# Two-layer graph attention and mixture-of-experts kernel: dense expert products summed from PSUM, nine result buffers, and another order of turns and results at the end

## The chip, the cores and the metric

The kernel runs on one core of a Trainium2 chip. The metric is device time in microseconds (us), the median over several executions. The engines are TensorE (PE, matrix products; PEld is its weight load), VectorE (DVE), ScalarE (ACT), GpSimd (POOL) and SyncE (SP). Each runs its own instructions in order and waits on semaphores for the others. SP issues the plain transfers, POOL the indirect ones (rows chosen by an index).

## What is computed

The input is 64 batches of 256 rows of 256 numbers in float32. Two layers follow each other, each an attention over a fixed graph of 256 nodes and then a feed-forward part:

```python
x = x + elu(attention_4_heads(layernorm(x), adj))     # layer 0
x = x + layernorm(x) @ weight.T + bias
x = x + relu(attention_1_head(layernorm(x), adj))     # layer 1
t = layernorm(x)                                      # tokens, 16384 rows
probs = softmax(t @ router_w.T)                       # 8 experts
rw, re = top_k(probs, 2); rw = rw / rw.sum()
out = t
for e in range(8):
    h = gelu(t @ w1[e] + b1[e])
    out = out + combine[:, e] * (h @ w2[e] + b2[e])   # combine: rw at re, else 0
return x + out
```

## The kernel before

**Batches.** Each batch passes through the attention and feed-forward parts in SBUF (`batch_layers`). At its end it has the normalized rows `xng`, and `base`, the sum of x and the normalized rows, to which the two chosen experts' outputs are still to be added.

**Routed batches.** For 62 of the 64 batches `base` is written to the output in DRAM (L585). The rows are sorted by expert: after a chunk of batches `route` sends every row, with its index and weights, by an indirect DMA to a region of its expert in the DRAM scratch `xs` (L877). Rows are then taken from there in pairs of blocks, 256 rows of one expert each: 131 pairs in all. `expert_pair` loads a pair's rows `xr` (L726) and their indices and weights `xt` (L737), and the expert's first weight matrix `we` (L752); DVE turns the rows blockwise into `sT` (L116, `turned`); `hidden` makes `hT` = gelu of the first product (PE L783, ACT L789); `result` makes the second product `py` in a PSUM bank (L798) and DVE adds the bias into a buffer `y` (L804); ACT scales it by each row's weight (L776). `scatter` adds the two halves of `y` to the output's rows by two indirect DMAs with addition on POOL's queue (L815). Each of them waits for the two of the pair before (`before = added[-2:] + based`), since two pairs can hold the same row. A buffer `y` is free when its scatter has landed.

**Dense batches.** The last two batches (62 and 63) aren't sorted. All 8 experts are computed on all of their rows (`dense_expert`, 16 in all): `hidden`, `result` into a buffer `y`, and then two DVE operations which multiply `y` by the rows' weight for this expert and add it to `base` in SBUF (L843). After the last expert `base` is written out (L850); for batch 63 that write waits for all scatter-adds, as filling rows of incomplete pairs point at its rows.

**Order.** The order of all instructions is written out by hand. Work is cut into pieces by generators: each `yield r` ends a piece and gives the rank r of the next one. The program goes in steps; in each step every active job gives one piece, in order of rank (a negative rank asks for another piece in the same step). Every third step begins a batch; in the steps between, pairs (two for each batch while batches still begin, `more`; three afterwards) and dense experts (two each third step) begin. One scatter is placed per step, at rank 97. A pair begun in step a loads in step a, loads `we` in a+1 (rank 90), is turned in a+2 (rank 95), goes through `hidden` in a+4 (rank 30), through `result` in a+5 (rank 80), and is scaled in a+6. So the turns of one group of pairs fall in the same step as the results of the group before.

**Buffers.** `WBUFS, XBUFS, YBUFS` are the counts of buffers for `we`, `xr` and `y`. `me` (the masked scores of layer 1, written by ACT at L432, read by DVE at L443) has the work pool's 2, `lg` (router scores of a chunk, L603) has 10, `xt` 12, and `w` (the rows' weights) 8.

Of the kernel before, what the change touches and what calls it, by code (L numbers as in the profile page):

```python
# [9 lines left out]
F32 = mybir.dt.float32  # L10
I32 = mybir.dt.int32
AF = mybir.ActivationFunctionType
ALU = mybir.AluOpType
AX = mybir.AxisListType

P = 128
# [11 lines left out]
def kernel(  # L28
# [17 lines left out]
    nc = tc.nc  # L46
    B, N, D = x.shape
    E = router.shape[0]
# [3 lines left out]
    NT = N // P  # L52
# [16 lines left out]
    ROW = D + 4  # L69
# [4 lines left out]
    work = ctx.enter_context(tc.tile_pool(name="work", bufs=2))  # L74
    small = ctx.enter_context(tc.tile_pool(name="small", bufs=4))
    keep = ctx.enter_context(tc.tile_pool(name="keep", bufs=1))
# [170 lines left out]


    C_B1, WROW = KT * D, KT * D + 64
    WBUFS, XBUFS, YBUFS = 7, 5, 7  # L250
    wpack = tc.dram_tile([E, P, WROW], F32, name="wpack")
    w2s = const.tile([P, E, KT * D], F32, tag="w2s", name="w2s")
    b2s = const.tile([P, E, D], F32, tag="b2s", name="b2s")
# [158 lines left out]
    def projected1(xT, rstd, b):  # L412

        q = q1s[b % 2]
        pqs = []
        for t in range(NT):
            pq = bank("pq", [D + 3])
            for k in range(KT):
                nc.tensor.matmul(  # L419
                    pq, xT[:, k, t * P : (t + 1) * P], wx1[:, k, :],  # L420
                    start=(k == 0), stop=(k == KT - 1),
                )
            pqs.append(pq)
        ex = small.tile([P, NT, 3], F32, tag="ex1", name="ex1")
        for t, pq in enumerate(pqs):
            nc.scalar.activation(ex[:, t, :], pq[:, D:], AF.Exp, scale=rstd[:, t : t + 1])
            nc.scalar.activation(
                q[:, t, :D], pq[:, :D], AF.Copy, scale=rstd[:, t : t + 1]
            )
        me = work.tile([P, NT, N], F32, tag="me", name="me")  # L430
        for j in range(NT):
            nc.scalar.activation(me[:, j, :], masks[1][:, j, :], AF.Copy, scale=ex[:, j, 0:1])  # L432
        return q, ex, me
# [276 lines left out]
    def expert_pair(j, n, ids, ef, regs, needs):  # L710

        i = j % GROUP
        upto = min(j + GROUP, n)
        if i == 0:
            _, regs["e"] = nc.values_load_multi_w_load_instructions(
                ids[0:1, 0, j:upto], engines=[mybir.EngineType.SP], min_val=0, max_val=E - 1,
                skip_runtime_bounds_check_because=WHY,
            )
            _, regs["t"] = nc.values_load_multi_w_load_instructions(
                ids[0:1, 1, j:upto], engines=[mybir.EngineType.SP], min_val=0, max_val=E * CAP,  # L720
                skip_runtime_bounds_check_because=WHY,
            )
        e_sp, t_sp = regs["e"][i], regs["t"][i]
        xr = io.tile([P, PAIR // S, KT * S], F32, tag="xr", name="xr", bufs=XBUFS)
        loads = [
            nc.sync.dma_start(  # L726
                out=xr[g * S : (g + 1) * S],
                in_=xs_d.rearrange("(t c q) f -> t q c f", c=PAIR // S, q=S)[
                    bass.ds(t_sp, 1), :, :, g * KT * S : (g + 1) * KT * S
                ].rearrange("t q c f -> (t q) c f"),  # L730
            )
            for g in range(P // S)
        ]

        xt = small.tile([P, 2, ROW - D], F32, tag="xt", name="xt", bufs=12)
        loads.append(
            nc.sync.dma_start(  # L737
                out=xt,
                in_=xs_d.rearrange("(t k p) c -> t p k c", p=P, k=2)[
                    bass.ds(t_sp, 1), :, :, D:  # L740
                ].rearrange("t p k c -> (t p) k c"),
            )
        )
        for load in loads:
            tc.add_to_no_dep_group("rows", load.ins)
            for name in needs:
                tc.add_manual_dep(
                    load.ins, name, AFTER, reason="any sent row may lie in the pair"
                )
        yield 90  # L750
        we = io.tile([P, WROW], F32, tag="we", name="we", bufs=WBUFS)
        nc.sync.dma_start(  # L752
            out=we, in_=wpack[bass.ds(e_sp, 1), :, :].rearrange("e p c -> (e p) c")
        )
        yield 95
        xT = turned(work.tile([P, KT, PAIR], F32, tag="sT", name="sT", bufs=3), xr)
        w = small.tile([P, 2], F32, tag="w", name="w", bufs=8)
        yield 30
        yield 30
        hT = hidden(xT, we)  # L760
        yield -65
        nc.vector.scalar_tensor_tensor(
            w[:, :, None], xt[:, :, 1:2], ef[:, j : j + 1], xt[:, :, 2:3],
            op0=ALU.is_equal, op1=ALU.mult,
        )
        nc.vector.tensor_tensor(w[:, :, None], w[:, :, None], xt[:, :, 3:4], ALU.add)
        yield 80
        if i == 0:
            _, regs["x"] = nc.values_load_multi_w_load_instructions(
                ids[0:1, 0, j:upto], engines=[mybir.EngineType.PE, mybir.EngineType.DVE],  # L770
                min_val=0, max_val=E - 1, skip_runtime_bounds_check_because=WHY,
            )
        y = result(hT, bass.ds(regs["x"][i], 1))
        yield 2
        for t in range(2):
            nc.scalar.activation(y[:, t, :], y[:, t, :], AF.Copy, scale=w[:, t : t + 1])  # L776
        scatters.append((y, xt))
# [13 lines left out]
            )  # L791
        return hT

    def result(hT, e):
        py = bank("py", [2, D])
        for t in range(2):
            for f in range(KT):
                nc.tensor.matmul(  # L798
                    py[:, t, :], hT[:, f, t * P : (t + 1) * P],
                    w2s[:, e, f * D : (f + 1) * D].rearrange("p e c -> p (e c)"),  # L800
                    start=(f == 0), stop=(f == KT - 1),
                )
        y = io.tile([P, 2, D], F32, tag="y", name="y", bufs=YBUFS)
        nc.vector.tensor_add(y, py, b2s[:, e, :].to_broadcast([P, 2, D]))  # L804
        return y
# [25 lines left out]
    def dense_expert(b, e):  # L831

        own = dense_batch[b]
        yield 90
        we = io.tile([P, WROW], F32, tag="we", name="we", bufs=WBUFS)
        nc.sync.dma_start(out=we, in_=wpack[e])
        yield 40
        yield 30
        hT = hidden(own["xT"], we)
        yield 80  # L840
        y = result(hT, slice(e, e + 1))
        for t in range(NT):
            nc.vector.scalar_tensor_tensor(  # L843
                own["base"][:, t, :], y[:, t, :], own["w"][:, t, e : e + 1],
                own["base"][:, t, :], op0=ALU.mult, op1=ALU.add,
            )
        if e == E - 1:
            while b == B - 1 and (scatters or len(added) < 2 * PAIRS):
                yield 99
            d = nc.sync.dma_start(  # L850
                out=out_rows[b * N : (b + 1) * N, :].rearrange("(t p) d -> p t d", p=P),
                in_=own["base"],
            )
            before = added[-2:] + based if b == B - 1 else []
            tc.declare_no_dep(
                d.ins, query=SYNC, group="out", keep=before,
                reason="no row is added to here, or every add is in their chain",
            )
            for ins in before:
                tc.add_manual_dep(d.ins, ins.name, AFTER, reason="filling rows were added here")  # L860
            tc.add_to_no_dep_group("out", d.ins)
            nc.sync.nop()
# [153 lines left out]
    def jobs():  # L1016
        b = done = taken = 0
        for c, nb in enumerate(CHUNKS + (1,) * DENSE):
            nt = nb * NT
            lg = keep.tile([P, nt, E], F32, tag="lg", name=f"lg_{c}", bufs=10)  # L1020
            xng = []
            row0 = b * N
            done += nt
            n = max(done - (E - 1) - taken, 0) if b < ROUTED else 0
            taken += n
            for i in range(nb):
                def job(b=b, c=c, i=i, nb=nb, nt=nt, n=n, lg=lg, xng=xng, row0=row0):
                    yield from batch_layers(b, i * NT, xng, lg)
                    if i == nb - 1:
                        if b >= ROUTED:  # L1030
                            yield 65
                            yield from route_dense(b, lg)
                        else:
                            yield from route(c, row0, nt, n, b == ROUTED - 1, xng, lg)
                yield job()
                b += 1

    batches = jobs()
    step, more, credit = 2, True, 0.0
# [74 lines left out]
```

## Time and profile before

| | us |
|---|---|
| median of 3 runs | 1666.84 |
| lowest and highest | 1666.26, 1670.07 |
| the profiled execution | 1670.08 |
| its span, first to last instruction | 1668.3 |

| engine | busy us | share of the span |
|---|---|---|
| PE | 1495.5 | 90% |
| PEld | 1311.2 | 79% |
| DVE | 1317.4 | 79% |
| POOL | 889.4 | 53% |
| ACT | 833.2 | 50% |

The transfers move 209.74 MB in 365285 packets, of which 264376 are under 512 bytes. The largest groups of transfers are the pairs' rows (524 of 64 KB), the experts' weights (147 of 288 KB), the scatter-adds (262) and the sends (248).

In lines in order of time the first number is the start in us from the start of the span, the second the duration; in brackets stands how long the engine was idle before, and what released it. Releasers are inferred from semaphore events: for a wait on several semaphores the last one is named, and it need not be the one that mattered. L12 is line 12 of the kernel. In a list of waits the numbers are the sum in us, the number of waits and the longest one.

### The profile page before, as it was taken

The numbers are of one execution on the slowest core, as the hardware profiler recorded it, in microseconds if no ns is written. First come the engines' busy times: TensorE is split into PE (matmuls) and PEld (weight loads), VectorE is DVE, ScalarE is ACT, GpSimd is POOL, SyncE is SP. The second block draws the span as 40 slices with busy tenths as digits, with TensorE's granted clock in tenths as the row PEclk, the third lists the DMA queues.
The fourth block names the chain that finished last, engine by engine and source line by source line (L and its number), as shares of the span: only waits on it lengthen the run. The fifth ranks groups of instructions, "written<-read, shape, count | busy, mean of one in ns | idle before, by whom it ended". The sixth has DMA issues, their size and how long they took to land.

```text
span 1668.3 us, 30242 instructions
## 1 busy us (share of the span) xinstructions
PE 1495.5 (90%) x8474; PEld 1311.2 (79%) x8474; DVE 1317.4 (79%) x4478; ACT 833.2 (50%) x1832; POOL 889.4 (53%) x853
## 2 busy tenths in 40 slices
PE   5898888899999999999999999999989987678782
PEld 4777777688888888888888888888878876567671
DVE  6888989999898988898989898998889876423330
ACT  0243444455656666666666665655555565323221
POOL 0121433545757575757575757574764666444344
PEclk8999999999999999999999999999999998879986
DMA  3812223255757575756575766665564676866753
GB/s 107 231 41 58 61 70 94 74 142 114 167 118 163 118 159 129 140 132 146 133 149 134 145 133 146 137 140 121 123 142 99 115 156 141 200 135 112 155 107 44
DMA packets 365285, 209.74 MB, mean 126 GB/s; under 512 B 264376, under 2 KB 335040, under 8 KB 365120
## 3 DMA queue, kind: packets, MB, share of 16 engines
q1 hardware_dynamic: 314496, 139.43, 34.0%
q0 software_dynamic: 49632, 67.39, 22.5%
q8 instruction: 70, 1.15, 0.3%
q10 hardware_dynamic: 992, 0.99, 0.2%
q14 instruction: 95, 0.78, 0.2%
HBM read 118.55 MB, written 89.15 MB: 124 GB/s over the span
## 4 chain that ended last, share of the span: by engine, by line
PE 55%; DVE 26%; DMA 6%; issue 5%; POOL 4%; ACT 2%; SPq 1%; DVEq 0%; POOLq 0%; ACTq 0%
PE ph L783 14%; PE pv L475 12%; PE py L798 9%; PE pq L384 5%; PE pq L419 4%; DVE z L461 4%; PE pf L529 4%; DVE stats L353 4%; DMA out_dram<-y,xt 3%; PE pt L368 3%; POOL out_dram L815 2%; DVE mv L354 2%; PE pl L599 2%; PE pd L454 1%; DVE x L535 1%
## 5 line engine op out<-in xcount | busy, mean ns | idle before, releaser
L815 POOL DMA_INDIRECT out_dram<-y,xt x262 | 416.7, 1591 | 255.4 <-DMA out_dram<-y,xt 73.0
L475 PE MATMUL pv<-q,z 128*128 128x65 f32 (+1 forms) x2560 | 369.8, 299 | 6.7 <-DVE z L461 5.3
L475 PEld LDWEIGHTS pv<-q,z 128*128 128x128 f32 x2560 | 331.9, 194 | 19.5 <-DVE z L461 5.8
L783 PE MATMUL ph<-sT,we 128*128 128x256 f32 x1048 | 259.1, 405 | 56.2 <-DVE sT L116 47.1
L361 POOL TENSOR_SCALAR rstd<-mv 128x4 f32<-128x4 f32 (+1 forms) x132 | 69.7, 528 | 436.1 <-DVE mv L354 352.9
L877 POOL DMA_INDIRECT xs<-xng,pos x248 | 251.1, 1012 | 69.2 <-issue 66.9
L783 PEld LDWEIGHTS ph<-sT,we 128*128 128x128 f32 x1048 | 209.8, 205 | 90.9 <-DVE sT L116 50.6
L798 PE MATMUL py<-w2s,hT 128*128 (+1 forms) x1176 | 263.9, 379 | 1.4 <-DVE z L461 0.7
L798 PEld LDWEIGHTS py<-w2s,hT 128*128 128x128 f32 x1176 | 219.7, 190 | 29.7 <-DVE z L461 1.0
L374 ACT COPY xT<-pt 128x512 f32<-128x512 f32 x192 | 113.3, 590 | 222.4 <-PE pt L368 184.7
L804 DVE TENSOR_TENSOR y<-py,b2s 128x512 f32<-128x512 f32 x147 | 97.5, 688 | 158.9 <-PE py L798 88.7
L789 ACT ACTIVATE hT<-ph,we 128x256 f32<-128x256 f32 x294 | 122.8, 471 | 183.3 <-PE ph L783 80.9
L461 DVE SCALAR_TENSOR_TENSOR z<-pd,q,mask 128x256 f32<-128x256 f32 x512 | 211.1, 473 | 0.3 <-PE pd L454 0.2
L362 POOL TENSOR_TENSOR rstd<-rstd,mhalf 128x4 f32<-128x4 f32 (+1 forms) x132 | 162.6, 1232 | 11.0
L776 ACT ACTIVATE y<-y,w 128x256 f32<-128x256 f32 x262 | 113.1, 501 | 104.4 <-DVE y L804 96.3
L353 DVE BATCH_NORM_STATS2 stats<-x 128x6 f32<-128x256 f32 x384 | 156.3, 407 | 2.2
L384 PE MATMUL pq<-wx,xT 128*128 128x268 f32 x512 | 137.9, 415 | 8.6 <-DVE wt L257 4.2
L419 PE MATMUL pq<-wx,xT 128*128 128x259 f32 x512 | 129.1, 394 | 15.5 <-ACT xT L374 11.2
L529 PE MATMUL pf<-wfT,xT 128*128 128x256 f32 x512 | 125.0, 388 | 0.0
L419 PEld LDWEIGHTS pq<-wx,xT 128*128 128x128 f32 x512 | 91.9, 189 | 41.9 <-ACT xT L374 22.4
L384 PEld LDWEIGHTS pq<-wx,xT 128*128 128x128 f32 x512 | 100.9, 202 | 30.1 <-issue 6.9
L551 ACT ACTIVATE rel<-pv,rinv 128x256 f32<-128x256 f32 x128 | 54.0, 474 | 108.2 <-DVE rinv L482 95.8
(151 smaller groups left out, 2233.8 us busy)
## 6 DMA issues: line engine op xcount, KB each, us to landing
we<-wpack SPq DMA_DIRECT2D x147, 288.0 KB
xr<-xs SPq DMA_DIRECT2D x524, 64.0 KB
xblk<-in_x_dram SPq DMA_DIRECT2D x256, 64.0 KB
xin<-in_x_dram SPq DMA_DIRECT2D x64, 256.0 KB
out_dram<-base SPq DMA_DIRECT2D x64, 256.0 KB
out_dram<-y,xt POOLq DMA_INDIRECT x262
xs<-xng,pos POOLq DMA_INDIRECT x248
xs<-fill SPq DMA_DIRECT2D x9, 260.0 KB
```

The source lines that it names most:

```text
L353: nc.vector.bn_stats(stats[:, t, :], src[:, t, :])
L362: nc.gpsimd.tensor_tensor(rstd[:, :n], rstd[:, :n], mhalf[:, :n], ALU.pow)
L384: nc.tensor.matmul(pq.rearrange("p h c -> p (h c)"), xT[:, k, t * P : (t + 1) * P], wx[:, k, :], start=(k == 0), stop=(k == KT - 1),)
L419: nc.tensor.matmul(pq, xT[:, k, t * P : (t + 1) * P], wx1[:, k, :], start=(k == 0), stop=(k == KT - 1),)
L461: nc.vector.scalar_tensor_tensor(z[:, j, :], pd[:, i, :], q[:, j, h, d + 2 : d + 3], mask[:, j, :], op0=ALU.max, op1=ALU.mult,)
L475: nc.tensor.matmul(pv[:, h, :], z[:, j, t * P : (t + 1) * P], q[:, j, h, : d + 1], start=(j == 0), stop=(j == NT - 1),)
L529: nc.tensor.matmul(pf[:, t, :], xT[:, k, t * P : (t + 1) * P], wfT[:, k, :], start=(k == 0), stop=(k == KT - 1),)
L783: nc.tensor.matmul(ph[:, f, :], we[:, k * D + f * P : k * D + (f + 1) * P], xT[:, k, :], start=(k == 0), stop=(k == KT - 1),)
L789: nc.scalar.activation(hT[:, f, :], ph[:, f, :], AF.Gelu, bias=we[:, C_B1 + f : C_B1 + f + 1])
L798: nc.tensor.matmul(py[:, t, :], hT[:, f, t * P : (t + 1) * P], w2s[:, e, f * D : (f + 1) * D].rearrange("p e c -> p (e c)"), start=(f == 0 ...
L815: d = nc.gpsimd.indirect_dma_start(out=out_rows, out_offset=bass.IndirectOffsetOnAxis(ap=xt[:, t, 0:1].bitcast(I32), axis=0), in_=y[:, t, ...
L877: d = nc.gpsimd.indirect_dma_start(out=xs_d[: E * CAP * PAIR, :], out_offset=bass.IndirectOffsetOnAxis(ap=at, axis=0), in_=xe, in_offset=None,
```

## The change

- `dense_expert` takes the second product straight from PSUM: in place of one add of the bias into `y` and two weighted sums from `y`, there are four weighted sums, two from the PSUM bank and two from the bias rows. No dense expert takes a buffer `y`. The matrix products are split off from `result` into `product`.
- `YBUFS` goes from 7 to 9.
- The turn of a pair has rank 75 in place of 95 once no batch is left to begin, so it comes ahead of the results (rank 80) of the same step.
- The write of a dense batch's `base` comes one step later, at rank 99.
- `me` has 1 buffer in place of 2, `lg` 7 in place of 10, `xt` 14 in place of 12, `w` 12 in place of 8.

```diff
-    WBUFS, XBUFS, YBUFS = 7, 5, 7
+    WBUFS, XBUFS, YBUFS = 7, 5, 9
...
-        me = work.tile([P, NT, N], F32, tag="me", name="me")
+        me = work.tile([P, NT, N], F32, tag="me", name="me", bufs=1)
...
-        xt = small.tile([P, 2, ROW - D], F32, tag="xt", name="xt", bufs=12)
+        xt = small.tile([P, 2, ROW - D], F32, tag="xt", name="xt", bufs=14)
...
-        yield 95
+
+        yield 95 if more else 75
         xT = turned(work.tile([P, KT, PAIR], F32, tag="sT", name="sT", bufs=3), xr)
-        w = small.tile([P, 2], F32, tag="w", name="w", bufs=8)
+        w = small.tile([P, 2], F32, tag="w", name="w", bufs=12)
...
-    def result(hT, e):
+    def product(hT, e):
         py = bank("py", [2, D])
...
+        return py
+
+    def result(hT, e):
+        py = product(hT, e)
         y = io.tile([P, 2, D], F32, tag="y", name="y", bufs=YBUFS)
         nc.vector.tensor_add(y, py, b2s[:, e, :].to_broadcast([P, 2, D]))
         return y
...
-        y = result(hT, slice(e, e + 1))
-        for t in range(NT):
-            nc.vector.scalar_tensor_tensor(
-                own["base"][:, t, :], y[:, t, :], own["w"][:, t, e : e + 1],
-                own["base"][:, t, :], op0=ALU.mult, op1=ALU.add,
-            )
+        py = product(hT, slice(e, e + 1))
+        for t in range(NT):
+            for add in (py[:, t, :], b2s[:, e, :]):
+                nc.vector.scalar_tensor_tensor(
+                    own["base"][:, t, :], add, own["w"][:, t, e : e + 1],
+                    own["base"][:, t, :], op0=ALU.mult, op1=ALU.add,
+                )
         if e == E - 1:
+            yield 99
             while b == B - 1 and (scatters or len(added) < 2 * PAIRS):
                 yield 99
...
-            lg = keep.tile([P, nt, E], F32, tag="lg", name=f"lg_{c}", bufs=10)
+            lg = keep.tile([P, nt, E], F32, tag="lg", name=f"lg_{c}", bufs=7)
```

## The prediction

> **What bounds the kernel now.** I read the table of windows first, for where the engines stop being full; then POOL and DVE in order of time over the last 260 us; then the waits and the DMA queues of that stretch.
>
> ```profile
> 800.00:1000.00 200.00, 197.85 (x1180) 177.09 (x1179) 180.07 (x594) 124.39 (x270) 127.00 (x120) 1.00 0.63 136
> ...
> 1450.00:1500.00 50.00, 31.10 (x122) 25.93 (x121) 13.60 (x33) 9.94 (x24) 21.65 (x14) 0.80 0.67 127
> ```
>
> The columns after the length are busy us of PE, weight load, DVE, ACT and POOL, then clock, DMA share and GB/s. Until about 1330 us TensorE is full (99% here). The tail is another regime: PE is busy 31 of 50 us, DVE 14, and nothing looks full. What does bound it is in POOL's order of time:
>
> ```profile
> 1494.28 1.54 POOL L815 DMA_INDIRECT out_dram<-y,xt  x1 [3.48 <-DMA xr<-xs]
> 1496.13 1.54 POOL L815 DMA_INDIRECT out_dram<-y,xt  x1 [0.31 <-issue]
> 1502.73 1.54 POOL L815 DMA_INDIRECT out_dram<-y,xt  x1 [5.06 <-ACT hT L789]
> ...
> 1625.64 1.54 POOL L815 DMA_INDIRECT out_dram<-y,xt  x1 [3.15 <-DMA out_dram<-y,xt]
> 1627.48 1.54 POOL L815 DMA_INDIRECT out_dram<-y,xt  x1 [0.30 <-issue]
> 1632.08 1.54 POOL L815 DMA_INDIRECT out_dram<-y,xt  x1 [3.05 <-ACT hT L789]
> ...
> 1658.29 1.54 POOL L815 DMA_INDIRECT out_dram<-y,xt  x1 [2.99 <-DMA out_dram<-y,xt]
> ```
>
> Two of these lines are one pair's scatter-add. The code makes each wait for both of the pair before it (L811 to L825: `before = added[-2:]`), so pairs form a chain. Uncontended a link takes 1632.08 - 1625.64 = 6.44 us (1.54 + 0.30 + 1.54 issued, 3.05 to land); beside loads it takes up to 8.45 (1494.28 to 1502.73) or 9.61. Is the chain ever short of data? DVE's order tells:
>
> ```profile
> 1614.28 0.69 DVE L804 TENSOR_TENSOR y<-py,b2s 128x512 f32<-128x512 f32 x1 [11.58 <-PE py L798]
> ...
> 1632.43 0.69 DVE L804 TENSOR_TENSOR y<-py,b2s 128x512 f32<-128x512 f32 x1 [6.81 <-PE py L798]
> 1634.21 0.69 DVE L804 TENSOR_TENSOR y<-py,b2s 128x512 f32<-128x512 f32 x1 [1.09 <-PE py L798]
> 1635.94 0.69 DVE L804 TENSOR_TENSOR y<-py,b2s 128x512 f32<-128x512 f32 x1 [1.03 <-PE py L798]
> ```
>
> The last of 131 pairs is summed at 1635.94 and scattered at 1658.29. Counting both lists back from the end, every pair is ready long before its turn: the least lead from 1440 on is 11.4 us (summed 1614.28, scattered 1625.64; about 1.6 of it go to ACT's scaling). So the chain of adds is the bound from 1405 us on, and DVE and PE wait for it, not it for them:
>
> ```profile
> DVE y L804 <- DMA out_dram<-y,xt: 28.1, 8, 6.2
> ...
> PE ph L783 <- DVE sT L116: 37.2, 7, 9.8
> ```
>
> (waits of 1436 to 1606 us). Those 28.1 us are DVE waiting for a y buffer that a scatter still holds; the turns stand behind it and PE behind the turns. That the releaser column names ACT or a load in POOL's lines is only which event came last by inference.
>
> **What the Trainium skill says.** "DMA: Bandwidth & Descriptors", Issuing engines are not separate DMA queues: transfers of SP and POOL run on the same 16 engines and interleave. The trace agrees: links beside loads are longer. The same page, Rules for kernel authors: an accumulating DMA reads its destination and writes it later, so the next one on the same bytes must wait for its semaphore; the chain must stay, and the diff leaves it. "Perfetto Trace Analysis", Optimization Strategy: the same gap repeating can mean too few buffers; the 28.1 us agree, though here the engine with the gap isn't the one that binds.
>
> **The change part by part.** The chain's sum first. From 1436.73 to 1606.09 there are 23 links in 169.4 us. Links with no load in them take 6.36 to 6.61, mostly 6.45; 23 x 6.45 = 148.4, so loads cost 21.0 us there. The SP queue moved this meanwhile:
>
> ```profile
> q1 hardware_dynamic: 37149, 16.96, 42.0%
> ```
>
> so 21.0/16.96 = 1.24 us per MB, and link by link the excess follows the megabytes (none: 6.45; 0.76 MB: 7.18; 1.72 MB: 8.45; 1.88 MB: 9.61). After 1606 eight links take 52.2 us, then 10.0 us to the end of the span (issue, landing, the last base write). Before 1436 POOL alternates sends (4 x 1.3 us), rstd and scatters in one order that the diff doesn't touch.
>
> (1) *Dense products summed from PSUM.* 16 dense experts lose an add of 0.69 us each (-11.0) and gain two scalar-tensor-tensor of 0.48 (L843; L461 with a PSUM operand takes 0.473) each: 32 x 0.48 = +15.4. DVE gains 4.4 us of work in 170 us where it is 55 busy; PE's bank is held 1.9 rather than 0.7 us, out of 8 banks, with no waiter behind it for most of a round. On the path: 0. If this cover were gone, 4.4.
>
> (2) *Nine y buffers, none for dense.* Of seven, two were taken by dense experts in every round of 3 pairs and 2 experts. Now a sum waits only for the scatter nine pairs earlier: the 28.1 us go. In the whole time before 1400 the same wait is 4.5 us in 6 pieces, DVE being 90% and PE 99% busy; between 0 and -4.5, I take -2.
>
> (3) *Turns at rank 75 instead of 95 once all batches have begun* (the last block turn is at 1293.26). DVE's order in a round becomes 3 turns, 3 pair sums, 2 dense sums; PE then finds sT ready when its products end. Its bubbles before ph (37.2 us) go; a round needs 5.45 + 3.62 + 8.80 = 17.9 us of PE instead of the 21 to 23 us it takes. The last sum would come up to 35 us earlier than 1636. What is late next is the chain, already late: value 0. Between 1310 and 1405 the turns come 1.9 us earlier per round (three sums of 0.6); PE waited 1.67 and 5.79 us there, but POOL's fixed order of sends and scatters ends last: 0, at best -2.
> New wait: if a turn waits for its xr load, three pair sums and two dense ones queue behind it. Loads are issued 10 us or more before their turns (1490.43 for the turn of 1512.03), and the third xr load of a round is released by the first turn of the round before, a whole round ahead. Cost 0 while the 11.4 us lead covers it.
>
> (4) *`yield 99` before the base write of batch 62.* SP stood 14.8 us at L850 for the last dense sum, with two we loads, three pairs' xr and xt, and three we loads behind it. These go out earlier: 0 for the chain. For batch 63 the write still follows the last scatter.
>
> (5) *me with one buffer, lg with 7, xt 14, w 12.* ACT's next me waits for DVE's z of the batch before; over all 64 batches it starts at least 12.1 us after that z began: 0, and each us beyond would cost up to 62 us in all. lg is written and read on DVE alone, 7 chunks apart: 0. The longer xt and w rings remove waits of 0.4 us: 0.
>
> So the only way for (2) to (4) to reach the end is contention. All loads still run; they are squeezed into fewer us. If the price is per MB, as the links show, the 21 us stay, earlier. Bounds: a saturating price could save a third to all of it (-7 to -21); a queue that is never empty could cost half more (+10). I take 0.
> Sum against the profiled execution: 1670.08 - 2 = 1668; this one is 3.2 us above the median of the runs, so on the median 1666.84 - 2 = 1665.
>
> **Rivals.**
> *A, contention saturates:* 2.21 MB in one link (1421.19 to 1429.50) cost only 8.31 us, 1.86 over 6.45, 0.84 us per MB. If all 17 MB ran so, 21.0 becomes 14.3; -7, with (2) at its best -4.5: about 1655. For: those were large packets. Against: 9.61 us for 1.88 MB.
> *B, slower, turns that wait for loads hold the sums up:* place: DVE before three sums of each round in the tail. Per round 5 x 288 KB + 3 x 260 KB = 2.2 MB; the stretch 1436 to 1606 moved 0.1 MB per us, so at that rate a round is 22 us. With sums bound to the next round's loads and loads to the freed buffers, a round could become 24.5 us; 8 rounds x (24.5 - 21.5) = 24, less the 10 us of lead: +14, 1681. It decides from about 22.8 us per round. Against: DMA was at a share of 0.70, the loads waited for buffers, not the buffers for loads.
> *C, the rounds don't quicken* because loads bind them: the chain is fed all the same; no change, 1667.
>
> **How the numbers follow.** No change that shows (the forecast and C): 0.50, own range 1662 to 1671. A: 0.36, from 1645 to 1661. B: 0.14, from 1672 up. About 0.3% (5 us) is what a measurement of this kernel can tell from no change. Predicted 1665; the range goes down to 1650 (the inner part of A) and up to 1671, leaving out some 8% below and 12% above.
>
> **What would show it.** Right: 36 pairs of scatters still follow each other at a mean of about 7.1 us from 1405 on; PE's wait for sT gone; the last pair sum 20 us or more before 1636 while the last scatter stays near 1658; loads ended by about 1580; no wait of ACT before me. Wrong: a mean link under 6.9 (A), DVE waiting at L116 for xr and pairs ready less than 3 us before their scatter (B), or time won before 1330 us, where I see none but the 4.5 us.

## The result, and the profile after

| | before | changed |
|---|---|---|
| median, us | 1666.32 (10 runs) | 1669.78 (10 runs) |
| the profiled execution, us | 1670.08 | 1669.61 |
| its span, us | 1668.3 | 1667.8 |

The ratio is 1.0028, with a 95% interval of 1.0015 to 1.0041 (the quotient of the two medians is 1.0021); a second measurement on another chip (e15) gave 1.0028 again (1.0015 to 1.0041, 1673.59 against 1668.76 us). The change costs about 4 us: little, but clear of the noise. The two profiled spans don't show it, since the first profile of the kernel before is the slowest of these ten runs; a second one (experiment e8) has a span of 1661.7 us. Both run the same chain of adds at the end, and the first is 6 us late when it gets there.

So from here the stretch before the 94th pair's scatter, which varies from execution to execution, is kept apart from the chain that follows it. A *link* is the time from the first scatter of a pair to the first of the next. All 131 pairs were numbered in POOL's order of time.

| profile | 94th scatter at | 94th to last | 98th to last | excess per MB, 98th to last |
|---|---|---|---|---|
| before | 1386.2 | 272.1 | 237.1 | 1.16 |
| before, second profile (e8) | 1380.4 | 271.5 | 236.6 | 1.15 |
| changed | 1380.9 | 276.9 | 241.1 | 1.37 |
| changed, second profile (e15) | 1385.6 | 277.3 | 242.4 | 1.44 |

All times are us. The last column is the sum of the 33 links less 33 x 6.44 us, over the MB that SP's queue moved in them. The chain is 5 us longer in both profiles of the changed kernel, for the same bytes (20.8 MB against 20.9 and 21.2). That is the loss.

The windows of the changed kernel, with the columns as before (PE, weight load, DVE, ACT, POOL, clock, DMA share, GB/s):

```profile
800.00:1000.00 200.00, 197.86 (x1181) 177.04 (x1180) 180.10 (x594) 124.39 (x270) 127.12 (x120) 1.00 0.62 136
1450.00:1500.00 50.00, 50.00 (x233) 44.03 (x232) 21.84 (x49) 18.47 (x44) 19.74 (x14) 1.00 0.79 167
```

The batches run as before. In the tail PE is busy 50 of 50 us where it was 31, and the DMA share rises from 0.67 to 0.79: the rounds did quicken. The waits from 1436 to 1606 us, by engine and line:

```profile
DVE y L809 <- DMA out_dram<-y,xt: 79.2, 14, 8.6
...
DVE sT L116 <- DMA xr<-xs: 7.0, 3, 3.8
```

PE's wait for turned rows (37.2 us before) isn't in the list any more. DVE waits longer for y buffers, 79.2 us in place of 28.1: results now run ahead until no buffer is free. The last sum and the last scatter of the changed kernel, in order of time on DVE and on POOL:

```profile
1604.99 0.69 DVE L809 TENSOR_TENSOR y<-py,b2s 128x512 f32<-128x512 f32 x1 [5.65 <-DMA out_dram<-y,xt]
```

```profile
1657.81 1.54 POOL L820 DMA_INDIRECT out_dram<-y,xt  x1 [3.10 <-DMA out_dram<-y,xt]
```

The last pair is summed 31 us earlier than before (1635.94), and scattered 53 us later. Everything in front of the chain was quickened, and the chain is slower. Its links in the middle of the tail, on POOL:

```profile
1526.58 1.54 POOL L820 DMA_INDIRECT out_dram<-y,xt  x1 [3.00 <-DMA out_dram<-y,xt]
1528.43 1.54 POOL L820 DMA_INDIRECT out_dram<-y,xt  x1 [0.30 <-ACT y L777]
1536.69 1.54 POOL L820 DMA_INDIRECT out_dram<-y,xt  x1 [6.71 <-DMA xr<-xs]
1538.54 1.54 POOL L820 DMA_INDIRECT out_dram<-y,xt  x1 [0.30 <-issue]
1543.17 1.54 POOL L820 DMA_INDIRECT out_dram<-y,xt  x1 [3.09 <-DMA out_dram<-y,xt]
1545.02 1.54 POOL L820 DMA_INDIRECT out_dram<-y,xt  x1 [0.30 <-ACT hT L790]
1549.65 1.54 POOL L820 DMA_INDIRECT out_dram<-y,xt  x1 [3.09 <-DMA out_dram<-y,xt]
```

One link takes 10.11 us (1526.58 to 1536.69), the next two 6.48 each. SP's queue at the same time:

```profile
1520.11 1.86 SPq L726 DMA_DIRECT2D xr<-xs  x4
1525.86 0.39 SPq L737 DMA_DIRECT2D xt<-xs  x1
1526.50 1.53 SPq L752 DMA_DIRECT2D we<-wpack  x3
1528.14 0.83 SPq L841 DMA_DIRECT2D we<-wpack  x2
1531.66 1.93 SPq L726 DMA_DIRECT2D xr<-xs  x4
1536.00 0.40 SPq L737 DMA_DIRECT2D xt<-xs  x1
1536.95 1.86 SPq L726 DMA_DIRECT2D xr<-xs  x4
1542.46 0.40 SPq L737 DMA_DIRECT2D xt<-xs  x1
```

SP waits at `xt` (45.7 us in 14 pieces from 1436 to 1606), whose 14 buffers come free only when a scatter lands; then all five weight loads of a round (5 x 288 KB) go out within 2.5 us, at the very start of a link. The long link carries 1.74 MB and costs 3.7 us over 6.44, 2.1 us per MB. The two others carry one pair's rows each (0.27 MB), issued while the two scatters of the link are still being issued, and cost nothing.

In the kernel before, links of 1.69 to 1.88 MB cost 1.5 to 3.2 us. The one from 1494.28 to 1502.73, which the prediction shows, carries 1.72 MB and costs 2.0. SP's queue at that time:

```profile
1490.43 1.90 SPq L726 DMA_DIRECT2D xr<-xs  x4
...
1493.23 2.28 SPq L752 DMA_DIRECT2D we<-wpack  x3
1496.90 2.07 SPq L836 DMA_DIRECT2D we<-wpack  x2
1499.22 1.91 SPq L726 DMA_DIRECT2D xr<-xs  x4
```

The written order is the same, and the bytes on the link are too, but here the five weights take 5.7 us to go out (1493.23 to 1498.97), in two groups.

### The profile page after: what moved, and what is told of

It is laid out like the page before. It is cut to its first block, busy times and chain, and to the rows that moved or that the text cites. A ratio compares the mean times of both kernels' runs of the same rounds, so it can differ in the third digit from the quotient of the medians.

```text
span 1667.8 us, 30267 instructions
## 1 busy us (share of the span) xinstructions
PE 1482.4 (89%) x8474; PEld 1303.1 (78%) x8474; DVE 1320.7 (79%) x4494; ACT 828.8 (50%) x1832; POOL 889.4 (53%) x853
## 3 DMA queue, kind: packets, MB, share of 16 engines
q8 instruction: 70, 1.15, 0.3%
## 5 line engine op out<-in xcount | busy, mean ns | idle before, releaser
L799 PE MATMUL py<-w2s,hT 128*128 (+1 forms) x1176 | 270.0, 386 | 17.6 <-DVE base L849 9.8
L799 PEld LDWEIGHTS py<-w2s,hT 128*128 128x128 f32 x1176 | 223.4, 194 | 49.0 <-ACT hT L790 17.8
L784 PE MATMUL ph<-sT,we 128*128 128x256 f32 x1048 | 241.1, 385 | 11.6 <-DVE sT L116 7.1
L784 PEld LDWEIGHTS ph<-sT,we 128*128 128x128 f32 x1048 | 198.6, 193 | 38.6 <-DVE sT L116 7.3
L809 DVE TENSOR_TENSOR y<-py,b2s 128x512 f32<-128x512 f32 x131 | 85.7, 684 | 106.1 <-DMA out_dram<-y,xt 83.7
L354 DVE BATCH_NORM_AGGREGATE mv<-stats 128x2 f32<-128x6 f32 x512 | 93.3, 182 | 17.5
```

The source lines that it names most:

```text
L784: nc.tensor.matmul(ph[:, f, :], we[:, k * D + f * P : k * D + (f + 1) * P], xT[:, k, :], start=(k == 0), stop=(k == KT - 1),)
L799: nc.tensor.matmul(py[:, t, :], hT[:, f, t * P : (t + 1) * P], w2s[:, e, f * D : (f + 1) * D].rearrange("p e c -> p (e c)"), start=(f == 0 ...
```

## The experiments

All ratios are to the kernel before on the same chip, with their 95% intervals. The sums of links are from one profile of each experiment. Where a kernel was profiled twice or more (before, changed, the late spread), its links from the 94th pair on agree within 0.7 us.

### Which part of the change: e1, e2, e4, e8

Only the turns:

```diff
-        yield 95
+        yield 95 if more else 75
```

> The kernel before, with the one change that pairs are turned at rank 75 once no batch is left. Theory L (locked loads: in the changed kernel SP waits for a free xt, which a landing scatter gives, so that the five weight loads of a round fall in one burst on one link of the scatter chain): dense experts still take y buffers, so the lead stays below the 12 xt and SP isn't held there; links as before, ratio 0.999 to 1.001, and no big link over 9.0 us in the steady rounds. Theory R (running ahead itself packs the same bytes on fewer links and each MB costs more): the rounds quicken a little, ratio 1.000 to 1.002. Theory N (smaller me and lg rings cost in the main part): 1.000.

Measured: 1.0008 (0.9998 to 1.0017); 94th to last 274.2 us, 2.4 above the mean of the two profiles of before; in time the loss isn't clear of the noise. Two links of the steady rounds take 9.76 and 9.11 us, which theory L had excluded.

Only the dense sums, with the buffers that they need:

```diff
-    WBUFS, XBUFS, YBUFS = 7, 5, 7
+    WBUFS, XBUFS, YBUFS = 7, 5, 9
...
-        y = result(hT, slice(e, e + 1))
+        py = product(hT, slice(e, e + 1))
...
+            for add in (py[:, t, :], b2s[:, e, :]):
```

> The kernel before, with the dense products summed from PSUM, nine y buffers and the me and lg rings of the changed kernel that make room for them; turns at rank 95, xt 12. Theory L: nine y buffers for pairs alone let the lead grow to the 12 xt, SP waits at xt for over 30 us, ratio 1.002 to 1.004. Theory R: the same without need of a wait at xt, ratio 1.001 to 1.003. Theory N: 1.002 to 1.004, lost before 1400 us.

Measured: 1.0019 (1.0003 to 1.0035); 94th to last 273.4 us (+1.6). SP waited 22.3 us for xt (from 1400 on), not over 30 as theory L had it; theory R's range holds. Not in this kernel, nor tested alone, are the later write of `base` and the longer xt and w rings.

Only the smaller rings of me and lg:

```diff
-        me = work.tile([P, NT, N], F32, tag="me", name="me")
+        me = work.tile([P, NT, N], F32, tag="me", name="me", bufs=1)
...
-            lg = keep.tile([P, nt, E], F32, tag="lg", name=f"lg_{c}", bufs=10)
+            lg = keep.tile([P, nt, E], F32, tag="lg", name=f"lg_{c}", bufs=7)
```

> The kernel before with one me and seven lg, nothing else. Theory N: ratio 1.002 to 1.004, the loss spread over the batches. Theories L and R, and the prediction: 0.999 to 1.001.

Measured: 1.0000 (0.9991 to 1.0009); 272.5 us. Theory N falls: the rings are free.

The kernel before once more, unchanged:

> The kernel before once more, for a second profile. If the 5.5 us by which its first profile ran behind the changed kernel's at the 89th pair (1342.0 against 1336.5) were chance, this one has its 89th pair at 1335 to 1338, its links from the 98th at 236 to 238.5 us and a span near 1662 to 1664. If the change had quickened the main part, it is at 1342 again.

Measured: one execution, 1663.55 us; its 89th pair is at 1336.0, its links from the 98th sum to 236.6. So the late start of the first profile doesn't belong to the kernel. Most of it arises at one place, where DVE stands still for 4.10 us in the first profile and not in the second:

```profile
1159.56 1.89 DVE L804 TENSOR_TENSOR y<-py,b2s 128x512 f32<-128x512 f32 x3 [4.10 <-PE pd L438]
```

The changed kernel has this wait too in its second profile (e15, 4.1 us) and not in its first. In the six of all 19 profiles that have it the 81st pair is at 1248.1 to 1252.3, in the others at 1242.6 to 1246.3. What it waits for wasn't found out.

Together: turns and dense sums each lengthen the chain (2.4 and 1.6 us; e4, whose tail is that of the kernel before, stands at 0.7), and with both it is 5 us longer. Each lets results, and so loads, run further ahead: the last weights go out 219 us after the 94th scatter in the kernel before, 209 in e1, 202 in e2 and 193 in the changed kernel.

### Is it SP's wait for xt, or the lead: e3, e5

```diff
-        xt = small.tile([P, 2, ROW - D], F32, tag="xt", name="xt", bufs=14)
+        xt = small.tile([P, 2, ROW - D], F32, tag="xt", name="xt", bufs=19)
```

> The changed kernel with 19 xt in place of 14. Theory L: SP's waits for xt (46 us in the changed kernel) fall to under 10 us, loads no longer start with a scatter, the big links of 9.3 to 10.1 us fall to about 8.3, and the ratio to before is 0.998 to 1.001. Theory R: loads run further ahead still, the same bytes lie on fewer links, ratio 1.002 to 1.004. Theory N: 1.002 to 1.004.

Measured: 1.0019 (1.0011 to 1.0027), 277.7 us. SP's waits from 1436 to 1606 in this kernel:

```profile
SPq L752 <- ACT hT L790: 25.7, 7, 9.5
SPq L857 <- DVE w L767: 8.7, 1, 8.7
...
SPq L726 <- DMA we<-wpack: 5.8, 8, 1.0
```

The wait for xt is gone, and SP waits for weight buffers (L752) instead; the links of over 1.2 MB still take 9.14 us in the mean (9.26 in the changed kernel). Theory L, that the wait for xt makes the loss, falls: the chain is as long without it.

```diff
-    WBUFS, XBUFS, YBUFS = 7, 5, 9
+    WBUFS, XBUFS, YBUFS = 7, 5, 5
```

> The changed kernel with 5 y buffers in place of 9, so that results can lead their scatters by 5 pairs only; dense sums, turns and the late base write stay. Theory R (running ahead packs the same bytes on fewer links of the chain, and a MB costs more where a link carries more): the lead is about that of the kernel before, the links from the 98th to the last sum to 237 to 238.5 us (before 237.1, changed 241.1), ratio to before 0.999 to 1.001. Theory Q (the loss lies in the dense sums from PSUM, the order of turns or the late base write, not in the lead): 1.002 to 1.004.

Measured: 1.0012 (1.0004 to 1.0020), 98th to last 239.1, 94th to last 274.3 us: between both theories' numbers. Half of the loss goes with the lead, though the changed kernel's order stays. A lead of five pairs still fed the chain (from the 94th on every pair was summed 19 us or more before its scatter).

e3 and e5 show one thing more. Five weights in one burst aren't needed: three, issued 0.7 us apart and 1.7 to 3.1 us after the start of a link, make links of 1.06 to 1.27 MB that cost 2.0 to 2.7 us: 1.9 to 2.1 us per MB, as much as the burst. What these links share with it is weights close behind each other.

### The loads on SP's queue in another order: e6, e7, e9 to e12

The order of a round in the changed kernel is: rows of three pairs, three weights, two dense weights. The spread order puts weights between rows:

```diff
+        late = not more
+        if late:
+            pair_no[0] += 1
+            yield (90, 91, 93)[(pair_no[0] - 1) % 3]
...
-        yield 90
+        if not late:
+            yield 90
         we = io.tile([P, WROW], F32, tag="we", name="we", bufs=WBUFS)
...
-        yield 95 if more else 75
+        yield 75 if late else 95
...
-                for _ in range(2):
+                for rank in (90, 92):
                     if dense_jobs:
-                        begin(dense_jobs.pop(0)(), 90)
+                        begin(dense_jobs.pop(0)(), rank)
```

> The changed kernel with the order of loads on SP's queue altered once no batch is left: each pair's weights directly behind its rows, and the two dense experts' weights between the pairs, in place of all five weights behind three pairs' rows. The same bytes, 0.55 to 0.85 MB on each link. Theory R: with links of 0.62 MB at 0.56 us over 6.44 and of 1.79 MB at 2.75 us (six profiles taken together), a round loses 1 us or more, the links from the 98th sum to 231 to 236 us, ratio 0.995 to 0.999. Theory C (a MB costs the same wherever it falls, as the prediction had it): 1.002 to 1.004, as the changed kernel.

Measured: 1.0028 (1.0019 to 1.0038), a miss as a time; but the links from the 98th sum to 236.3 us, as expected. The loss moved: 87.0 us from the 89th to the 98th pair where the changed kernel has 80.2. The rows come one step later in this order, and DVE waited for them at L116, 62.4 us from 1400 on and 13.0 us before, while batches still ran on it.

The same order only once the first dense batch is routed, with the changed kernel's rule for the turns:

```diff
-        late = not more
+        late = dense_on[0]
...
-        yield 75 if late else 95
+        yield 95 if more else 75
...
         dense_batch[b]["w"] = w
+        dense_on[0] = True
```

> The changed kernel with the spread order of loads only from the time on that the first dense batch is routed; up to there loads, turns and sends stand as in the changed kernel. Theory R (a MB costs more on a link that carries more): the 8 us that the earlier spread lost between the 89th and the 98th pair are gone (80 us there, as in the changed kernel), and the links from the 98th on sum to 234 to 238 us (changed 241.1, earlier spread 236.3); ratio to before 1.000 to 1.0015. Theory C (the same price wherever it falls): 240 to 242, ratio 1.002 to 1.0035.

Measured: 0.9982 (0.9972 to 0.9993), 1661.6 us; 98th to last 233.9, 94th to last 268.2 us. The chain is 8.7 us shorter than in the changed kernel and 3.6 shorter than before, and the time lower than either theory had it. POOL and SP of this kernel in the middle of the tail:

```profile
1517.21 1.54 POOL L827 DMA_INDIRECT out_dram<-y,xt  x1 [4.16 <-DMA out_dram<-y,xt]
...
1524.93 1.54 POOL L827 DMA_INDIRECT out_dram<-y,xt  x1 [4.33 <-ACT y L784]
...
1533.69 1.54 POOL L827 DMA_INDIRECT out_dram<-y,xt  x1 [5.38 <-DMA xr<-xs]
...
1540.93 1.54 POOL L827 DMA_INDIRECT out_dram<-y,xt  x1 [3.85 <-DMA out_dram<-y,xt]
```

```profile
1523.65 0.36 SPq L847 DMA_DIRECT2D we<-wpack  x1
1524.20 1.88 SPq L732 DMA_DIRECT2D xr<-xs  x4
1526.35 0.40 SPq L743 DMA_DIRECT2D xt<-xs  x1
1526.99 0.35 SPq L759 DMA_DIRECT2D we<-wpack  x1
1527.46 0.41 SPq L847 DMA_DIRECT2D we<-wpack  x1
1528.11 1.96 SPq L732 DMA_DIRECT2D xr<-xs  x4
```

Rows and weights alternate. Links of 1.35, 1.82 and 0.96 MB take 7.72, 8.76 and 7.24 us: 0.8 to 1.3 us per MB (the two after them 1.4 and 1.5), where the burst paid 2.1; over all 33 links it is 0.96. The last weights go out at 1563.6, 10 us before the changed kernel's (1573.7). So it isn't running ahead as such that costs, which theory R had said at first: here the loads end sooner and cost less.

Each expert's first weights loaded once for both dense batches, on the changed kernel and on the late spread:

```diff
-        we = io.tile([P, WROW], F32, tag="we", name="we", bufs=WBUFS)
-        nc.sync.dma_start(out=we, in_=wpack[e])
+        if b == ROUTED:
+            dense_we[e] = io.tile([P, WROW], F32, tag="we", name="we", bufs=WBUFS)
+            nc.sync.dma_start(out=dense_we[e], in_=wpack[e])
+        we = dense_we[e]
...
-        dense_jobs.extend(lambda e=e: dense_expert(b, e) for e in range(E))
+        if b == B - 1:
+            dense_jobs.extend(
+                lambda e=e, d=d: dense_expert(d, e) for e in range(E) for d in range(ROUTED, B)
+            )
```

> The changed kernel with the dense experts of batches 62 and 63 run side by side, so that each expert's first weights are loaded once for both: 8 loads of 288 KB (2.36 MB) fewer. Theory R: they come out of the big bursts, 1.5 us for each MB, so 3.5 us less, the links from the 98th sum to about 237, ratio 0.999 to 1.001. Theory C: 1.2 us for each MB, 2.8 us less, ratio 1.000 to 1.002. Theory Q: the same as the changed kernel, 1.002 to 1.004.

On the late spread:

> The same, and each expert's first weights loaded once for both dense batches: 2.36 MB fewer. Theory R: at a price of about 1.1 us for each MB, 2.4 us less than the spread alone, links from the 98th 232 to 236 us, ratio 0.998 to 1.000. Theory C: 1.2 us for each MB, 238 to 239, ratio 1.0005 to 1.002.

Measured: e7 1.0014 (1.0005 to 1.0022), 94th to last 273.7 us, 3.2 less than the changed kernel, a time that theory C covers and theory R doesn't. e10 **0.9967 (0.9953 to 0.9980), 1660.60 us**, 266.3 us, 1.9 less than the late spread, and again lower than expected. On this chip it beats both kernels; its lead over the late spread (1660.60 against 1661.60 us) isn't clear of the noise. Bytes that are never loaded come off the chain.

The filling writes in four groups, on top of e10:

```diff
                 nc.sync.nop()
+                if e % 2:
+                    yield 95
```

> The same, and the eight filling writes (2.1 MB, which lie on one link of 10.4 us in the changed kernel) issued in four groups of two, a step apart. Theory R: that link falls to about 8 us and two or three others grow by 0.3 us, 1 to 2 us less, ratio 0.997 to 0.999; if the later filling holds the flush pairs' loads back, the same as without. Theory C: no difference from the shared and spread kernel.

Measured: 0.9970 (0.9957 to 0.9983), 266.9 us: no difference from e10. In e10 the filling writes are already issued half on each of two links, of 7.8 and 8.9 us, where the changed kernel has the one of 10.4; in e11 they lie on three, of 7.3, 7.6 and 8.9 us.

The late spread on the kernel before:

> The kernel before with the spread order of loads from the time on that the first dense batch is routed; seven y buffers, dense sums through y, turns behind results. Theory R: its big links (8.4 to 9.3 us) shrink, links from the 98th sum to 233 to 236 us (before 236.6 and 237.1), ratio 0.998 to 1.000. Theory C: 1.000; and if weights that are ordered behind xr loads that wait for turns come late to PE, 1.001 or more.

Measured: 1.0001 (0.9988 to 1.0013), 273.1 us, 98th to last 238.8. A miss: of its links of 0.84 to 1.23 MB five cost 1.7 to 2.0 us, three 0.9 to 1.2. SP's waits from 1415 on:

```profile
SPq L759 <- PE ph L790: 38.1, 5, 15.5
```

With seven y buffers and turns behind results, SP stands at a weight load until PE's products free a buffer, and what follows goes out at once. The same written order fell on the links in another way. MB per link alone doesn't set the price.

### Weights together, or rows a step later: e13, e14

The late spread kept, with the five weights of a round put together again:

```diff
-            yield (90, 91, 93)[(pair_no[0] - 1) % 3]
+            yield 90
...
-        if not late:
-            yield 90
+        yield -92 if late else 90
...
-                for rank in (90, 92):
+                for rank in (94, 94):
```

> The late spread with one thing put back: a round's five weight loads stand together again behind its three pairs' rows; the delay of the loads by one step and all else stay as in the late spread. Theory W (what costs is that the weights of a round fall on one link): big links of 9 to 10 us return, the links from the 94th pair to the last sum to 274 us or more (changed kernel 276.9, late spread 268.1), ratio to before 1.001 to 1.003. Theory D (the delay of the loads by a step did it, through DVE's waits for rows): links as in the late spread, ratio 0.997 to 0.9995.

> The late spread with 19 xt in place of 14. Theory L (SP's wait for a free xt sets how the loads fall on the links): SP's waits for xt (6.2 us in 4 pieces in the late spread) go and the links change; ratio 0.002 off the late spread's 0.998 to one side or the other. Theory W: the order of the loads alone matters, the same as the late spread, 0.997 to 0.9995.

Measured on one chip: e13 1.0050 (1.0035 to 1.0065), 274.6 us, 98th to last 240.4; e14, the late spread with 19 xt, 1.0003 (0.9992 to 1.0015), 268.9 us, 98th to last 234.6. POOL's links in e13:

```profile
1536.70 1.54 POOL L826 DMA_INDIRECT out_dram<-y,xt  x1 [4.66 <-ACT hT L796]
...
1546.25 1.54 POOL L826 DMA_INDIRECT out_dram<-y,xt  x1 [6.16 <-DMA xr<-xs]
```

and SP's queue in them:

```profile
1538.02 1.47 SPq L758 DMA_DIRECT2D we<-wpack  x3
1539.76 0.68 SPq L846 DMA_DIRECT2D we<-wpack  x2
```

The link of 9.55 us is back as soon as five weights go out together, with rows as late as in the late spread. e13 is 5.7 us longer than e14 in the chain and 5.9 in the medians (1677.04 against 1671.13). Theory W holds on the chain and in this difference. But both ratios were above what it expected, e13's (1.001 to 1.003) as well as e14's, so the late spread, with 14 and 19 xt, and the changed kernel were measured on one chip:

> The changed kernel, beside the late spread with 14 and with 19 xt on one chip. All theories: ratio to before 1.002 to 1.004, links from the 94th pair to the last 275 to 278 us.

> The late spread with 14 xt. Theory W (the order of the weight loads alone matters): ratio to before 0.997 to 0.9995, 7 us or more below the changed kernel, links from the 94th 267 to 270 us, and the same as with 19 xt within 0.1%.

> The late spread with 19 xt. Theory W: the same as with 14 xt within 0.1%; then the 1.0003 measured before belongs to that chip. Theory L (the xt ring has a part in it): 1.0003 again, 0.15% or more above 14 xt.

Measured: changed 1.0028 (1.0015 to 1.0041), 277.3 us; late spread with 14 xt 1.0001 (0.9989 to 1.0014), 268.6 us; with 19 xt 1.0000 (0.9988 to 1.0012), 268.7 us. The xt ring has no part. The chain repeats to 0.7 us; the late spread is 5.2 us below the changed kernel in the medians (1668.41 against 1673.59) and 8.7 in the profiles. Against the kernel before its chain is 3 us shorter, which one chip's medians show (0.9982) and the other's don't (1.0001). Where those 3 us stay, ahead of the chain, is open. All five profiles of e13 to e17 have DVE's wait of 4 us near 1160 that was shown with e8, and none of e1 to e12 has it; as the kernel before wasn't profiled on those chips, this is a place to look and no more. e10 wasn't run there.

## Why the prediction was right and wrong

The measured 1669.78 us lies inside the range of 1650 to 1671, but the kernel became slower where a small gain was forecast.

- **The chain of adds is the bound of the tail: right.** 131 pairs follow each other as before; their last results were ready 53 us ahead.
- **(1) Dense sums cost DVE work that nobody waits for: right for the path,** the chain having no wait for DVE. It had said that PSUM banks have no waiter; PE now waits 9.8 us in 3 pieces for the dense sums (L849), at no cost to the end. That the sums let loads run ahead is part of (2).
- **(2) The -2 us before 1400 from nine y buffers: wrong.** The wait that they were to remove is 4.6 us in 6 pieces in the changed kernel, 4.5 before. Whatever held the sums there, two more buffers didn't free it. Nor did the 28.1 us of the tail go: they became 79.2, for which the chain doesn't wait.
- **(2) to (4): PE's bubbles go, the last sum comes 31 us earlier, SP's loads end sooner: right.** The last group of weights began to go out at 1572.5 (1603.4 before). That the last scatter stayed near 1658 was luck: the first profile of the changed kernel comes to the 94th pair 5.3 us earlier than that of the kernel before, and its chain is 4.8 us longer. No xr load held a turn for long (7.0 us in all), so rival B, slower because of late rows, wasn't the mechanism, although the sign was its own.
- **(5) Smaller rings cost nothing: right** (e4, 1.0000); ACT never waits for me. That a longer xt ring removes waits missed that SP comes to wait for xt (45.7 us); without this wait the loss is the same (e3).
- **The step that failed is the last: "If the price is per MB, as the links show, the 21 us stay, earlier. ... I take 0."** The links didn't show such a price: the prediction named four that rise in order, and the same list has others that don't.

```profile
1466.47 1.54 POOL L815 DMA_INDIRECT out_dram<-y,xt  x1 [3.63 <-ACT hT L789]
...
1473.67 1.54 POOL L815 DMA_INDIRECT out_dram<-y,xt  x1 [3.81 <-ACT hT L789]
...
1530.38 1.54 POOL L815 DMA_INDIRECT out_dram<-y,xt  x1 [3.06 <-DMA out_dram<-y,xt]
...
1539.35 1.54 POOL L815 DMA_INDIRECT out_dram<-y,xt  x1 [5.58 <-ACT hT L789]
```

The link from 1466.47 takes 7.20 us with 1.38 MB, that from 1530.38 takes 8.97 with 1.21 MB: 0.8 us over 6.44 against 2.5. The 1.24 us per MB was a mean over such links. With the rounds quickened the same bytes were issued otherwise, five weights in one burst at the start of a link and one pair's rows on each of the next two, and the mean went from 1.15 to 1.37 and 1.44 us per MB: +5 us on the chain where the sum has 0. With the weights spread it is 0.96 (late spread, again 0.94). The prediction's upper bound for this term, half more (+10), held the value. Rival A, a price that falls where loads are dense, is the opposite of what was found; its one link (2.21 MB in 8.31 us) carried 2.97 MB and took 10.59 us in the second profile of the same kernel.

So the sum's -2 should have been about +4 to +5. Shown: that weights standing together behind the rows cost the chain 6 us more than weights between the rows, in a kernel that runs ahead (e13 against e14), and that a shorter lead gives back half of the loss (e5). Not shown: why loads issued close together cost a scatter more for each MB, why the spread order gains nothing in the kernel before (e12), and where the 3 us of e16 stay.

## What to carry to other kernels

Where a serial chain of transfers is the bound, as here, engines that are quickened in front of it gain nothing, and what they trigger can slow it: ask at which moments of a link the other transfers will start. Don't take a price of contention from a mean per MB, nor from the links that fit it; look at all of them and at when their loads were issued. Try large loads kept apart by small ones between them on the queue, and look in the profile whether they really go out so: in e9 they did, in e12 the same written order did not. Number the links and compare the chain by itself before believing two spans; here the first profile's late start of 6 us hid a loss of 5.

## What the runs showed of the hardware

- In the changed kernel a pair's rows (four loads of 64 KB) issued from just before to 2 us after the start of a link cost that link nothing: 0.27 MB at 6.36 to 6.64 us, against 6.31 to 6.54 for links without loads (6.93 for the one of the 128th pair). In the kernel before, rows issued mostly 3.1 to 4.7 us after the start cost 0.5 to 0.6 us (0.26 to 0.30 MB at 6.91 to 7.00).
- Five loads of 288 KB issued within 3 us, most of them in the first 3 us of a link, made that link 2.8 to 3.7 us longer in the changed kernel's first profile (1.74 to 2.00 MB in all). Alternating with rows, as in the late spread, loads cost 0.94 to 0.99 us per MB over the last 33 links (four profiles), against 1.37 and 1.44 in the changed kernel.
